# A four-layer graph network on one core: the input sums of one fast-multiplication pair are placed earlier in layer 2, and the weight sums of the last layer are placed behind four layer norms

## The chip, the cores and the metric

The kernel is one program for one NeuronCore of a Trainium2 chip. The metric is the device time of one execution in microseconds. A core has five engines that run side by side, each working through its own queue in order: TensorE (PE, matrix products into PSUM, with weight loads listed as PEld), VectorE (DVE), ScalarE (ACT), GpSimd (POOL) and SyncE (SP), which here only issues DMA transfers. An engine that needs another's result waits on a semaphore, and everything behind the waiting instruction waits too.

## The reference

The input `x` has 128 graphs of 64 nodes with 256 features, with one adjacency matrix for all. Four layers follow each other, and each ends with `x = layernorm(x + layer(x))`:

```python
# layer 0: graph attention with a dense mask
Wh = x @ W;  e = leaky_relu(Wh@a1 [:,None] + Wh@a2 [None,:]);  h = softmax(where(adj, e, -inf)) @ Wh
# layer 1: edge attention over 512 edges (src, dst), 4 heads, softmax per source node, then @ W_out.T
# layer 2: normalised adjacency, two linear layers with batch norms over all 8192 rows
agg = A_hat @ features
h   = relu(batchnorm(agg @ W1.T + b1))          # 256 -> 512
out = batchnorm(h @ W2.T + b2)                  # 512 -> 256
# layer 3: two graph convolutions, then LSTMs over windows of 1, 2, 3 and 4 nodes, in this order
h = relu(adj @ (x @ Wg0 + bg0));  h = relu(adj @ (h @ Wg1 + bg1))
for p in 1..4:
    last = lstm(Wih[p-1], Whh[p-1], windows of p nodes of h);  h[:, last node of each window] = last
```

All arithmetic is in 32-bit floats.

## The kernel before

The 8192 rows are worked on in 16 blocks `q` of 512 rows (`QT`), kept transposed in SBUF as `Aq(q)`: two halves of 128 features by 512 rows.

*Layers 0 and 1* run in a loop over blocks. The last steps of layer 1 for a block are three functions. `v_a` multiplies the values by the attention weights. `v_b` multiplies by the output weights, adds the old rows (L463, on DVE), makes the layer norm (statistics on DVE, L95 and L96; the power -0.5 on POOL, L86; four scalings on POOL, L100) and stores the block (`x2_dram`, an SP transfer at L467). `v_c` multiplies by the normalised adjacency (64 small products, L482) and writes the input of layer 2 into `Aq(q)`.

*Layer 2's first linear layer* makes `Z = W1 Aq` and gathers its batch-norm statistics (`bn_stats` on DVE). Seven blocks and the block `q = 11` are done plainly by `up_block` (products at L789). Pairs of neighbouring blocks (7 and 8, 9 and 10, 12 and 13, 14 and 15) use seven instead of eight block products (a Winograd form of Strassen's scheme). `Seven` holds such a job: `product(j)` multiplies (L860) and `use` combines the result with kept ones (`kept`, L872, and L885 and L888 on DVE; L870, L874, L876 and L879 on ACT; L880 and L886 on POOL). The product numbered 4 belongs to `tail`, which `seven` weaves into the next job.

The scheme needs four sums of a pair's inputs, made by `tile_sums`: three on POOL (`t3`, `t2`, `t4`, at L116 in the profile because all pass through the helper `given`) and one on DVE, in place (`t1`, written into `Aq`). Each pair takes one of two `rooms` in turn; pair 12 takes `[gath, lb, keep]`, so that `t3` is `lb`, `t2` is `gath` and `t4` is `keep`. Pair 7 had the same room.

The nine steps that finish layer 1 (`v_a`, `v_b`, `v_c` for blocks 13, 14, 15) alternate with nine entries of `fill`: five plain blocks, then `pair(7, 0)`, `pair(7, 1)`, `pair(9, 0)`, `pair(9, 1)`. The sums of pair 7 are made after the step n = 3, those of pair 9 after n = 5. Pair 12's are made when the loop is over, ahead of `up_block(11)`. After the loop SP also loads layer 3's weights and biases (`wg`, `bg`, `wih`, `bias`, `bias2`) into rooms that layer 1 leaves, and DVE adds the two biases (L1189).

*Layer 3* begins with four blocks (`parts`, generators made by `gcn`) that step through scaling, transposition, layer norms (two for each block, each with two stores `x3_dram` at L1338 and an `x2r` load of a later block at L1019), the small products with the adjacency (`neighbours`, L1295) and two linear layers (L1365, L1377). `first_sums` makes, once, four sums of the first LSTM's input weights on POOL (L1412) for the same seven-product scheme, and stores them (`sums1`), since the room is used for other weights afterwards and later pairs of block groups load them again. A list of block numbers gives the order in which the generators take their steps; `first_sums` stands before the list.

*What sets the order.* `given(do, ...)` issues a step so that on each of PE, DVE, ACT and POOL it comes after the instructions of the steps issued through `given` before it. Everything not pinned in this way, SP's transfers among it, is placed by the framework's scheduler, from the order in the code and from when it expects operands to be ready.

## Time and profile before

| | |
|---|---|
| median of 3 runs | 2028.21 us (2027.94 to 2029.69) |
| profiled execution | 2025.54 us |
| its span, first to last instruction | 2023.8 us |
| granted TensorE clock, mean | 0.986 |
| PE busy | 1934.4 us (96%) |
| DVE, ACT, POOL busy | 1277.3, 951.1, 881.1 us |
| DMA | 173.83 MB, mean 86 GB/s |
| chain that ended last | PE 77%, DVE 14%, ACT 4% |

The span is counted from the first to the last instruction of the profiled execution; the execution's own time is 1.74 us longer. Busy time is what an engine spent in instructions; the chain that ended last is followed back from the last instruction to whatever released each step. The granted clock is the share of TensorE's full clock; where it falls to 0.5, a product takes twice as long. A time in a profile line is in us from the start of the span, its second number is how long the merged instructions took, and the bracket at the end tells how long the engine had been idle and who ended that.

Layer 1's last steps and layer 2's pairs lie at about 555 to 640 us, layer 3 begins at about 745 us, and the LSTM steps fill the rest from about 785 us.

### The profile page before, as it was taken

What the parts mean: (1) busy time and instruction counts of PE and PEld (TensorE: products, weight loads), DVE (VectorE), ACT (ScalarE), POOL (GpSimd) and SP (SyncE); (2) the same over time, 40 slices, a digit from 0 to 9 for tenths busy, and PEclk for the clock granted to TensorE, in tenths of its full rate; (3) what the DMA queues carried; (4) which work ended last, traced back from release to release, by engine and by line L of the source; (5) the groups of instructions that cost most, each with busy time, mean ns of one, the idle gap of its engine ahead of it and who ended that gap; (6) DMA issues with size and microseconds to landing.
All of it is one profiled execution on the core that took longest, in us unless ns stands there. A gap on an engine that the chain in (4) does not pass through costs nothing.

```text
span 2023.8 us, 31384 instructions
## 1 busy us (share of the span) xinstructions
PE 1934.4 (96%) x11447; PEld 1336.6 (66%) x11447; DVE 1277.3 (63%) x2855; ACT 951.1 (47%) x1666; POOL 881.1 (44%) x1020
## 2 busy tenths in 40 slices
PE   5999999998999989899999999999999999999997
PEld 4667777776554445477678577678577668578685
DVE  7567776664556554765566765557865557764566
ACT  2666656665346523644333644343644333543333
POOL 1133343343444632664545544445543445444264
PEclk8999999999999989999999999999999999999998
DMA  5344443332311134432342233133243032131022
GB/s 141 72 68 69 82 79 55 56 56 45 45 46 27 42 132 144 177 125 94 120 141 84 101 124 136 42 130 93 64 146 118 19 115 70 41 120 79 0 63 73
DMA packets 236539, 173.83 MB, mean 86 GB/s; under 512 B 150625, under 2 KB 213601, under 8 KB 233057
## 3 DMA queue, kind: packets, MB, share of 16 engines
q1 hardware_dynamic: 234528, 169.86, 29.6%
q8 instruction: 90, 1.47, 0.3%
q0 software_dynamic: 1024, 1.05, 0.2%
q10 hardware_dynamic: 832, 0.92, 0.1%
q14 instruction: 65, 0.52, 0.1%
HBM read 110.18 MB, written 61.60 MB: 85 GB/s over the span
## 4 chain that ended last, share of the span: by engine, by line
PE 77%; DVE 14%; ACT 4%; issue 2%; POOL 1%; DMA 1%; SPq 0%; DVEq 0%; POOLq 0%; ACTq 0%
PE l L1743 29%; PE l L1699 8%; PE pz L860 4%; PE l L1478 4%; PE m L338 3%; PE pz L789 3%; PE m L257 3%; PE e L367 3%; PE z L376 2%; PE m L461 2%; PE m L341 2%; PE g L1377 2%; PE g L1365 2%; PE pz L1058 2%; DVE cell L1657 1%
## 5 line engine op out<-in xcount | busy, mean ns | idle before, releaser
L1743 PE MATMUL l<-hs,wh 128*128 128x256 f32 (+1 forms) x896 | 276.0, 399 | 3.7 <-DVE hs L1607 3.1
L1743 PE MATMUL l<-xs,wx 128*128 128x256 f32 (+1 forms) x896 | 276.0, 399 | 2.8 <-DVE gate L1762 2.8
L1758 ACT ACTIVATE kept<-l 128x256 f32<-128x256 f32 (+1 forms) x224 | 88.6, 402 | 333.6 <-PE l L1743 332.2
L86 POOL TENSOR_TENSOR ln_rs<-ln_rs,mhalf 128x2 f32<-128x2 f32 (+2 forms) x98 | 85.9, 876 | 344.2 <-DVE ln_rs L98 338.6
L1743 PE MATMUL l<-H,wx 128*128 128x256 f32 (+1 forms) x672 | 210.5, 402 | 4.3 <-DVE gate L1771 3.4
L1743 PE MATMUL l<-hid,wh 128*128 128x256 f32 (+1 forms) x672 | 208.8, 399 | 0.0
L1743 PEld LDWEIGHTS l<-hs,wh 128*128 128x128 f32 x896 | 169.1, 190 | 47.1 <-DVE hs L1607 5.7
L1743 PEld LDWEIGHTS l<-xs,wx 128*128 128x128 f32 x896 | 168.9, 190 | 45.8 <-POOL st L100 2.7
L1699 PE MATMUL l<-H,wx 128*128 128x256 f32 (+5 forms) x672 | 185.0, 431 | 4.9 <-DVE H L116 2.7
L1776 ACT ACTIVATE gate<-gate,bias 128x512 f32<-128x512 f32 (+1 forms) x280 | 170.5, 657 | 40.6 <-DVE gate L1767 34.8
L378 ACT ACTIVATE u<-z 128x1024 f32<-128x1024 f32 x128 | 130.0, 1025 | 71.9 <-PE z L376 71.3
L1699 PEld LDWEIGHTS l<-H,wx 128*128 128x128 f32 x672 | 118.8, 190 | 65.3 <-issue 34.7
L1743 PEld LDWEIGHTS l<-H,wx 128*128 128x128 f32 x672 | 125.7, 190 | 42.6 <-DVE gate L1771 7.4
L1743 PEld LDWEIGHTS l<-hid,wh 128*128 128x128 f32 x672 | 127.2, 190 | 32.0 <-issue 2.9
L1766 POOL TENSOR_TENSOR gate<-gate,kept 128x256 f32<-128x256 f32 (+1 forms) x84 | 65.0, 774 | 145.3 <-DVE kept L1764 145.0
L1771 DVE TENSOR_TENSOR gate<-l,gate 128x256 f32<-128x256 f32 (+1 forms) x112 | 49.9, 446 | 87.6 <-POOL gate L1766 60.8
L349 DVE TENSOR_TENSOR qs<-m,qs 64x256 fp32r<-64x256 f32 x128 | 54.0, 422 | 76.5 <-ACT qs L348 74.4
L1611 POOL TENSOR_TENSOR hs<-hid 128x256 f32<-128x256 f32 (+1 forms) x28 | 26.0, 929 | 171.0 <-DVE hid L1643 87.9
L376 PE MATMUL z<-gath_r,qs 128*128 128x512 f32 x256 | 99.5, 477 | 0.6 <-ACT u L378 0.5
L1665 ACT ACTIVATE gate<-cell 128x512 f32<-128x512 f32 (+1 forms) x88 | 58.6, 666 | 82.6 <-DVE cell L1657 60.6
L1653 POOL TENSOR_TENSOR cell<-gate,cell 128x512 f32<-128x512 f32 (+1 forms) x56 | 75.3, 1366 | 28.2 <-ACT gate L1776 28.2
L1760 DVE TENSOR_TENSOR gate<-l,kept 128x256 f32<-128x256 f32 (+1 forms) x112 | 49.0, 438 | 59.9 <-ACT gate L1776 32.7
(386 smaller groups left out, 4079.4 us busy)
## 6 DMA issues: line engine op xcount, KB each, us to landing
wx<-sums SPq DMA_DIRECT2D x9, 2048.0 KB
wh<-sums SPq DMA_DIRECT2D x9, 1792.0 KB
way<-st SPq DMA_DIRECT2D x54, 256.0 KB
st<-way SPq DMA_DIRECT2D x216, 64.0 KB
xin<-in_x SPq DMA_DIRECT2D x16, 512.0 KB
ld<-table SPq DMA_DIRECT2D x16, 512.0 KB
x_dram<-y SPq DMA_DIRECT2D x16, 512.0 KB
x2r<-x_dram SPq DMA_DIRECT2D x32, 256.0 KB
```

What stands on the lines that cost most here:

```text
L86: nc.gpsimd.tensor_tensor(dst, dst, mhalf[:, :n], OP.pow)
L257: nc.tensor.matmul(p_, xT[:, k, c * P:(c + 1) * P], w0[:, k, :], start=k == 0, stop=k == KD - 1)
L376: nc.tensor.matmul(z[:, k, :], L1[q]["qs"][c][:, s, k * P:(k + 1) * P], gath_r, start=True, stop=True)
L378: nc.scalar.activation(u, z, AF.Relu)
L860: nc.tensor.matmul(self.bank[at], lhs, rhs, start=first and n == 0, stop=n == len(self.terms) - 1, skip_group_check=True)
L1478: nc.tensor.matmul(self.bank[at], lhs, rhs, start=new, stop=True, skip_group_check=True)
L1653: nc.gpsimd.tensor_tensor(c, t, c, OP.mult)
L1699: nc.tensor.matmul(b, w.raw[0][:, k, at, m, :], x, start=k == 0, stop=k == KD - 1)
L1743: nc.tensor.matmul(self.banks[j], lhs, rhs, start=src == 0, stop=src == 1)
L1758: nc.scalar.activation(self.keep(j), b, AF.Copy)
L1766: e.tensor_tensor(t[0][:, 1], t[0][:, 1], k[5], OP.add)
L1776: given(lambda: nc.scalar.activation(dst, dst, f, bias=b))
```

## The change

In layer 2, `tile_sums` is split: the generator `sums_in_two` issues `t3`, `t1` and `t2` in a first part and `t4` in a second, and `tile_sums` runs both at once for the pairs that keep their place. For pair 12 the first part is issued after the step n = 6 (`v_a` of block 15 and `pair(7, 1)`), the second after n = 7 (`v_b` of block 15 and `pair(9, 0)`). Later `T` takes over the finished list.

In layer 3, `first_sums` is issued after the seventh step in the list of block steps (the `None`), which is behind the first four layer norms; its store becomes a function of its own, `keep_sums`, and is called after the list.

```diff
-        def tile_sums(b):
+        def sums_in_two(b):
 
             t2, t3, t4 = rooms[next(rooms_at) % len(rooms)]
             t1 = b(0, 1)
             given(nc.gpsimd.tensor_tensor, t3, b(1, 1), t1, OP.subtract)
             given(nc.vector.tensor_sub, t1, t1, b(0, 0))
             given(nc.gpsimd.tensor_tensor, t2, b(1, 1), t1, OP.subtract)
+            yield
             given(nc.gpsimd.tensor_tensor, t4, b(1, 0), t2, OP.subtract)
-            return [t1, t2, t3, t4]
+            yield [t1, t2, t3, t4]
+
+        def tile_sums(b):
+            both = sums_in_two(b)
+            next(both)
+            return next(both)
...
             if n in sums_at:
                 T[sums_at[n]] = tile_sums(inputs(sums_at[n]))
+            if n == 6:
+                end_sums = sums_in_two(inputs(NQ - LAST))
+                next(end_sums)
+            elif n == 7:
+                T[NQ - LAST] = next(end_sums)
...
-        T = {ends[0]: tile_sums(inputs(ends[0]))}
+        T = {ends[0]: T[ends[0]]}
         given(up_block, q)
...
             nc.gpsimd.tensor_tensor(S[:, dst], x, y, op)
+
+    def keep_sums():
+        S = rooms_of(0)[1]
         d = dram.tile([P, 3 * QT], F32, name="sums1")
         nc.sync.dma_start(d, S.rearrange("p j g c -> p (j g c)"))
         sums_kept.append(d)
...
-    given(first_sums)
-    for n in [0, 0, 0, 1, 1, 0, 1, 0, 0, 1, 2, 0, 0, 2, 1, 2, 1, 0, 3, 1, 1, 1]:
-        given(next, parts[n])
+    for n in [0, 0, 0, 1, 1, 0, 1, None, 0, 0, 1, 2, 0, 0, 2, 1, 2, 1, 0, 3, 1, 1, 1]:
+        given(*(first_sums,) if n is None else (next, parts[n]))
+    keep_sums()
```

## The prediction

> **What bounds the kernel now.** I read the page first. TensorE is busy almost throughout and the chain that ended last is mostly its own work, so time can only be won where PE stands still or runs at a reduced clock.

> ```profile
> PE 1934.4 (96%) x11447; PEld 1336.6 (66%) x11447; DVE 1277.3 (63%) x2855; ACT 951.1 (47%) x1666; POOL 881.1 (44%) x1020
> PEclk8999999999999989999999999999999999999998
> ```

> Then I read the chain of waits around the end of layer 1 beside layer 2, where the diff moves `tile_sums`. Columns: start, length, who.

> ```profile
> 596.61 2.16 POOL y L100 x4
> 598.77 1.23 POOL lb L116
> ...
> 600.81 1.27 POOL gath L116
> 602.08 1.23 POOL Z L880
> 603.30 1.23 POOL keep L116
> 604.53 1.23 POOL Z L886
> ...
> 606.40 0.68 DVE kept L872
> ...
> 607.13 1.12 PE pz L860 x2
> ```

> POOL runs the last norm (`y`), and then the three sums of pair 12 (`lb`, `gath`, `keep`) interleaved with pair 9's additions (`Z`). The last addition releases a DVE statistic, that one DVE's `kept` sum, and that one the product `seg` on PE. PE's timeline shows 2.31 us of idle before 607.13, put down to `kept L872`. The stretches just behind it (length, busy us of PE, PEld, DVE, ACT, POOL, then the granted clock) show a second loss:

> ```profile
> 606.00:608.00 2.00, 0.87 (x2) 0.49 (x3) 1.97 (x4) 0.00 (x0) 1.86 (x3) 1.00 0.92 265
> 608.00:610.00 2.00, 2.00 (x4) 0.86 (x3) 1.64 (x3) 0.00 (x0) 1.98 (x3) 0.60 0.96 17
> 610.00:612.00 2.00, 2.00 (x4) 0.74 (x3) 0.70 (x1) 0.57 (x1) 2.00 (x2) 0.55 0.81 6
> ```

> The clock costs 0.40 x 2 + 0.45 x 2 = 1.7 us. Third, POOL's and PE's timelines at the start of layer 3:

> ```profile
> 748.45 1.97 POOL L1412 TENSOR_TENSOR wh<-wih 128x384 f32<-128x384 f32 x2 [1.98 <-PE g L1327]
> 750.49 0.99 POOL L1412 TENSOR_TENSOR wh<-wh,wih 128x384 f32<-128x384 f32 x1
> 751.57 0.99 POOL L1412 TENSOR_TENSOR wh<-wih,wh 128x384 f32<-128x384 f32 x1
> 752.52 0.70 POOL L86 TENSOR_TENSOR ln_rs<-ln_rs,mhalf 128x2 f32<-128x2 f32 x1
> ```
> ```profile
> 753.93 1.25 PE L1295 MATMUL g<-bdT,A 64*64 64x64 f32 x32 [3.47 <-POOL A L100]
> 755.82 1.25 PE L1295 MATMUL g<-bdT,A 64*64 64x64 f32 x32 [0.64 <-POOL A L100]
> ```

> `first_sums` (L1412) holds POOL for 4.1 us; the first norm's power stands behind it and PE waits 3.47 us for that norm.

> **Part 2, the sums of layer 3 behind four norms.** Same four POOL additions, moved. DVE's first L85 ran at 750.08 and took 0.36 us, ending with POOL's addition; alone it takes 0.17 (770.72). So the power can start at 750.35 instead of 752.52. It takes 0.70, and the two L100 (1.09) end at 752.25. The second norm was ready on DVE at 752.14; its L85 will again wait for POOL's L100 (to 752.25), so its power starts near 752.5, and its first L100 ends at 752.5 + 0.70 + 0.10 + 0.55 = 753.85, against 755.77 now. PE's second group of 32 moves from 755.82 to 753.9: **1.9 us**. From 755.82 to 800 PE is idle for less than 1 us in all, so nothing there takes it back. Norms three and four follow at 754.6 and 758.1; the four additions then fill 760 to 764, where POOL sat idle for 8.95 us (to 770.97) and will be wanted near 769. DVE's work in that stretch (L1367) read PSUM and took 0.69 beside a busy POOL at 761.70, so I charge nothing. If that cover failed, up to 4 us of the fifth norm's lead would go.

> On SP the store of the sums (0.32 us to issue) used to stand before eight `x_dram` stores, and the four `x2r` loads behind all eight. In the new order each pair of stores is followed by its load, then the sums' store (now waiting for POOL at 764), the load of `WhhT` (748.32 before, about 764 after), one `z_dram` load and the `x3r` loads. The `x2r` loads come up to 10 us earlier, but no wait of DVE or PE on them shows now, so that is worth nothing. `WhhT` is first needed by L1244 at 831.28: 60 us of cover. What queues behind the store until 764 was issued at 764.4 to 767.2 before.

> **Part 1, pair 12's sums two places sooner.** The same four subtractions. On POOL `lb` now stands between pair 7's two additions, `gath` after them, `keep` behind the norm. On DVE the subtraction in place stands before the two sums L463 of the last norm. Step by step:

> - POOL: L880 ends at 589.88 as now; `lb` 589.84 to 591.11; L886 from 591.07 (589.84 now).
> - DVE's subtraction is released by `lb` at 591.15, after POOL began L886. Both read two operands from SBUF. The nearest row for that:

> ```profile
> 841.35 2.38 DVE L116 TENSOR_TENSOR wh<-wh,hs 128x512 f32<-128x512 f32 x2 [0.19 <-ACT wh L116]
> ```
> ```profile
> 841.31 1.27 POOL L116 TENSOR_TENSOR gate<-wx,gate 128x512 f32<-128x512 f32 x1 [0.47 <-ACT wh L116]
> ```

> Two such DVE operations take 1.29 us alone (818.64) and 2.38 when POOL began 0.04 earlier: the first was held until POOL ended. So ours ends at 592.9. Behind it: L463, a statistic, L463, and the norm's statistics, now at 592.94, then at 594.65. The norm is 1.7 us late (d = 1.7). Bounds: not held, d = 0.6 (the statistic between the two sums still waits for L886 until 592.34); held by `gath` as well, which waits for it, is excluded. I take 1.7, by the row.
> - POOL's L100 ends at 600.5 instead of 598.77. PE's 64 products on `y` (598.00 to 599.28) end at 600.85: it waits about 1.6 us here.
> - Behind the norm only `keep` and the two `Z` additions are left: 600.5 + 3 x 1.23 = 604.2; statistic, then `kept` at 604.85, done 605.5. PE reaches `seg` at 600.8 + 5.25 (its present distance, 599.22 to 604.66, less a 0.1 wait) = 606.05. The stall is gone; `seg` runs 1.1 us sooner, the reduced clock saves 1.7: PE is 2.8 ahead.
> - What is late next:

> ```profile
> 613.14 0.19 DVE L1189 TENSOR_TENSOR bias<-bias,bias 128x32 f32<-128x32 f32 x1 [2.44 <-DMA bias<-in_L_gnn_bhh]
> ```

> DVE is in order, and this addition waits for two bias loads. SP issues them behind `x_dram<-y` (issued when the norm ends, 599.1) and `wih`, which waits until that store has landed (603.8); all of this moves by d, to 614.85. Behind the addition stand six statistics and sums of 0.6 and one of 0.77, and the next `kept`: 5.2 us, so 620.05. Now PE, not DVE, was late there (619.50). PE wants that `kept` for the product at 622.07 - 2.8 = 619.3 and gets it at 620.1. Then DVE's in-place subtraction and POOL's `wv` (1.26) let the product at 623.79 start at 622.0: **1.8 us** sooner, in general 3.55 - d.

> From there to 743 PE has one wait of 0.19 us, so 1.8 is kept. [...] The row has the fall behind 2.31 us (0.60, 0.55), and idles of 1.91 (133.04), 2.09 (78.46) and 2.24 (471.94) fell too, while 1.77 (830.06) did not. I go by the rows. By the same rows the new wait at 598 to 600.85, about 1.65 us in pieces, stays just below.

> **Sum.** 1.8 + 1.9 = 3.7 us. The profiled execution took 2025.54 (span 2023.8 and 1.74 outside); its successor would take 2021.8. The median of the runs lies 2.67 above it, which I carry over: 2028.21 - 3.7 = 2024.5.

> **Rivals.**

> - *The port does not hold DVE* (0.32), or the clock falls less often. d = 0.6: part 1 gives 2.9 and the sum 4.8: 2023.4, down to 2022 with one more window of full clock. For it: the hold rests on 0.08 us of order.
> - *Layer 2 gives nothing* (0.12). The broken wait at 598 drops the clock (up to 1.7 us, of which 0.7 is slack before the bias load decides), or the dip at 608 is missing in most runs of before. Then only part 2 counts: 1.9, 2026.3, to 2028 with a slow return of the clock in layer 3.
> - *The bias loads become the bound* (0.11, slower). Place: DVE's addition, now 613.14. Price: 1 us per us of delay, and 1.7 when PE stands long enough to lose its clock. Part 1 loses from d = 3.55, the whole change from about 3.8 (5.5 without the clock). For it: the loads move single elements (DMA 0.96 busy at 17 GB/s), and they are tied to a norm that this change delays. Against: nothing adds traffic there, and d is bounded by one POOL addition. With a delay of 10 us: 6.45 + 1.7 - 1.9 = 6.2 slower, 2034.4.
> - That the change does nothing is excluded: the order of POOL, DVE and SP differs as described; PE's and ACT's are unchanged.

> **Numbers.** The main case has 0.45, at 2024.5 (2023 to 2026). Over 0.2% (4.1 us, about what a measurement of this kernel can tell from no change) means below 2024.1: a third of the main case, nearly all of the first rival: 0.46. Slower by 0.2%: the bias case, 0.11. Between: 0.43. The range, 2022.0 to 2028.0, leaves out the bias case and the ends of the others.

> **What would show it.** `lb` near 590, before pair 7's last addition; DVE's subtraction beside it 1.75 us long (0.69: first rival); L100 ending at 600.5; no idle before `seg`; granted clock 1.00 from 606 to 612; DVE's bias addition near 614.9 and PE idle about 0.8 us before the `lb` product that follows. In layer 3: power at 750.4, L1295 near 751.8 and 753.9, 4 us of L1412's successors from 760. Wrong: a bias wait beyond 617, a reduced clock behind 601, or PE waiting for the fifth norm.

## The result, and the profile after

The changed kernel took 2020.34 us (median of 8 runs, 2017.79 to 2023.74), and the kernel before, run beside it, 2028.08 (8 runs, 2023.16 to 2030.43). The ratio is 0.9968, with a 95% interval of 0.9957 to 0.998: 4 to 9 us faster. The forecast was 2024.5, with a range down to 2022.0. The direction was right, the mechanisms in the main too, and the time lies below the range. The sections below put the change at 3 to 5 us, near the 3.7 of the forecast, and the usual time of before at about 2024.8 instead of the 2028.2 that the sum started from. In this first comparison before ran at 2028 all the same, and why is not shown.

The changed kernel's profiled execution took 2020.14 us (span 2018.4). The page, busy time and granted clock:

```profile
PE 1933.2 (96%) x11447; PEld 1337.6 (66%) x11447; DVE 1277.1 (63%) x2855; ACT 951.8 (47%) x1666; POOL 884.7 (44%) x1020
PEclk8999999999999989999999999999999999999998
```

PE's busy time fell by 1.2 us, the span by 5.4. Busy time alone would not show where: a product at half clock counts as busy for twice as long (in before, L789's products start 0.86 us apart at a granted clock of 0.5, at 608.62 and 609.48, and 0.43 us apart at full clock, at 612.36 and 612.79).

**A point of reference first.** The two profiles are already 1.92 us apart at pair 7's addition L880 (588.61 before, 586.69 after), ahead of every instruction that the change moves. The clock explains most of it. In the first 100 us the granted clock fell to 0.5 in before at 24.72, 38.38, 52.03 and 79.34 us, for 3.41 us each and 6.83 at 38.38, and in the changed kernel at 22.58 and 39.65, for 6.83 us each: 17.1 us in all against 13.7. The 3.41 us more cost up to 1.7 us, half of them, by my estimate. So below I give distances from two markers inside one profile: from pair 7's L880 on POOL for layer 2, and from the scaling's power (`sc`, L86 on POOL) for layer 3.

**Layer 2.** The chain of waits in the changed kernel (start, length, who):

```profile
587.96 1.24 POOL lb L116
...
589.26 1.63 issue
590.89 0.68 DVE y L463
...
596.35 2.18 POOL y L100 x4
...
604.78 7.78 DMA bias<-in_L_gnn_bhh
...
612.65 0.19 DVE bias L1200
...
617.84 7.37 PE pz L860 x16
```

In before this chain ran over POOL's additions, `kept` and `seg`. Those are gone from it. In their place stand the subtraction on DVE that is held (1.63 us in which nothing else shows), the norm, and behind `seg` the bias load. PE's timeline in before, then in the changed kernel, and the stretches behind `seg` (length, busy PE, PEld, DVE, ACT, POOL, granted clock, DMA):

```profile
607.13 1.12 PE L860 MATMUL pz<-seg,SW 128*128 128x512 f32 x2 [2.31 <-DVE kept L872]
608.09 3.30 PE L789 MATMUL pz<-A,w 128*128 128x512 f32 x4
...
623.79 1.02 PE L860 MATMUL pz<-wv,SW 128*128 128x512 f32 x2
```
```profile
596.96 2.07 PE L482 MATMUL m<-aht,y 64*64 64x64 f32 x64 [0.81 <-POOL y L100]
604.21 1.02 PE L860 MATMUL pz<-seg,SW 128*128 128x512 f32 x2
605.07 1.88 PE L789 MATMUL pz<-A,w 128*128 128x512 f32 x4
617.84 1.12 PE L860 MATMUL pz<-lb,SW 128*128 128x512 f32 x2 [0.32 <-DVE kept L872]
...
619.79 1.12 PE L860 MATMUL pz<-wv,SW 128*128 128x512 f32 x2
```
```profile
604.00:606.00 2.00, 2.00 (x6) 0.83 (x5) 1.97 (x4) 0.93 (x2) 1.92 (x3) 1.00 0.75 184
606.00:608.00 2.00, 2.00 (x6) 0.88 (x5) 0.78 (x2) 0.69 (x1) 2.00 (x3) 1.00 1.11 219
```

The 2.31 us of idle before `seg` are gone, and so is the clock of 0.60 and 0.55: L789's four products take 1.88 us instead of 3.30. PE now waits earlier, for the late norm, and later, before the product on `lb` (0.32). The wait for the norm is 0.81 us ahead of the 64 small products and goes on inside them: they start in groups of 16, each behind one of POOL's four scalings, 0.54 us apart instead of 0.28, so the merged line reads 2.07 us where before had 1.28. The granted clock is 1.00 there, and one product takes 0.22 us in both. From L880, `seg` starts at +17.52 (before +18.52) and the product on `wv` at +33.10 (before +35.18): 2.1 us.

**Layer 3.** The scaling's power and the first LSTM products in before:

```profile
745.93 0.54 POOL L86 TENSOR_TENSOR sc<-sc,mhalf 128x1 f32<-128x1 f32 x1 [6.32 <-DVE sc L85]
```
```profile
785.34 7.03 PE L1546 MATMUL l<-H,wih 128*128 128x512 f32 x16
```

POOL's and PE's timelines in the changed kernel:

```profile
742.06 0.54 POOL L86 TENSOR_TENSOR sc<-sc,mhalf 128x1 f32<-128x1 f32 x1 [6.32 <-DVE sc L85]
747.10 0.70 POOL L86 TENSOR_TENSOR ln_rs<-ln_rs,mhalf 128x2 f32<-128x2 f32 x1 [4.50 <-DVE ln_rs L98]
```
```profile
744.02 2.03 PE L1338 MATMUL g<-ident,A 128*128 128x128 f32 x8
...
748.51 1.66 PE L1306 MATMUL g<-bdT,A 64*64 64x64 f32 x32 [1.61 <-POOL A L100]
750.52 1.24 PE L1306 MATMUL g<-bdT,A 64*64 64x64 f32 x32 [0.35 <-POOL A L100]
...
779.90 7.03 PE L1560 MATMUL l<-H,wih 128*128 128x512 f32 x16
```

The first norm's power stands at +5.04 from the scaling's (before +6.59), the second group of small products at +8.46 (before +9.89), and the first product of the LSTM at +37.84 (before +39.41). So the profiles show 2.1 and 1.6 us at the two places, and 1.9 ahead of both that do not belong to the change.

### The profile page after: what moved, and what is told of

Same layout as the page of the kernel before. It is cut to its first block, busy times and chain, and to the rows that moved or that the text cites. A ratio compares the mean times of both kernels' runs of the same rounds, so it can differ in the third digit from the quotient of the medians.

```text
span 2018.4 us, 31386 instructions
## 1 busy us (share of the span) xinstructions
PE 1933.2 (96%) x11447; PEld 1337.6 (66%) x11447; DVE 1277.1 (63%) x2855; ACT 951.8 (47%) x1666; POOL 884.7 (44%) x1020
## 4 chain that ended last, share of the span: by engine, by line
PE 76%; DVE 14%; ACT 3%; DMA 2%; issue 2%; POOL 1%; SPq 0%; DVEq 0%; POOLq 0%; ACTq 0%
PE l L1757 27%; PE l L1713 8%; PE l L1492 4%; PE pz L860 4%; PE m L338 3%; PE e L367 3%; PE z L376 3%; PE m L257 3%; PE m L341 3%; PE pz L789 2%; PE m L461 2%; PE g L1388 2%; PE pz L1069 2%; PE g L1376 2%; PE l L1560 1%
## 5 line engine op out<-in xcount | busy, mean ns | idle before, releaser
L86 POOL TENSOR_TENSOR ln_rs<-ln_rs,mhalf 128x2 f32<-128x2 f32 (+2 forms) x98 | 86.4, 882 | 343.5 <-DVE ln_rs L98 331.3
```

The lines of the kernel that those rows point to most:

```text
L86: nc.gpsimd.tensor_tensor(dst, dst, mhalf[:, :n], OP.pow)
```

## The experiments

The measures of all profiles in one table; a session is a set of runs made side by side on one chip. "seg" and "wv" are the starts of these products after pair 7's L880, "clock" tells whether it was reduced behind `seg` (L789's four products took 1.88 us where it is called full, 2.55 to 3.36 where reduced), "LSTM" is its first product after the scaling's power. The ratio is to before in the same session, with its 95% interval; medians of before were 2024.54, 2024.35, 2024.88 and 2025.90 in four sessions (e1 to e4, e5 to e8, e9 to e12, e13), each on another chip.

| kernel | seg | wv | clock | LSTM | median us | ratio |
|---|---|---|---|---|---|---|
| before | 18.52 | 35.18 | reduced | 39.41 | | |
| changed | 17.52 | 33.10 | full | 37.84 | 2020.34 | 0.9968 (0.9957 to 0.998) |
| e1 part 1 alone | 17.51 | 33.04 | full | 38.56 | 2021.96 | 0.9986 (0.9979 to 0.9992) |
| e2 part 2 alone | 18.54 | 35.08 | reduced | 38.01 | 2023.38 | 0.9993 (0.9984 to 1.0001) |
| e3 before again | 18.51 | 35.17 | reduced | 39.38 | 2026.24 | 1.0004 (0.9994 to 1.0013) |
| e4 bias addition later | 17.52 | 32.38 | full | 38.06 | 2020.35 | 0.9978 (0.9967 to 0.9988) |
| e5 idle filled, 4 products | 19.67 | 35.13 | full | 39.31 | 2023.81 | 0.9998 (0.9989 to 1.0007) |
| e6 store alone | 18.53 | 35.19 | reduced | 38.81 | 2023.97 | 0.9997 (0.9989 to 1.0005) |
| e7 subtraction behind the norm | 16.77 | 31.73 | full | 36.48 | 2019.02 | 0.9971 (0.996 to 0.9982) |
| e8 layer 3 filled, 12 products | 17.52 | 32.38 | full | 37.82 | 2021.60 | 0.9988 (0.9981 to 0.9995) |
| e9 changed again | 17.51 | 32.57 | full | 37.72 | 2020.67 | 0.9976 (0.9966 to 0.9986) |
| e10 idle filled, 2 products | 18.52 | 35.13 | full | 39.26 | 2024.07 | 0.9998 (0.999 to 1.0006) |
| e11 layer 3 filled, 5 products | 17.51 | 32.37 | full | 36.18 | 2018.95 | 0.997 (0.9959 to 0.9982) |
| e12 e7 and e11 together | 16.79 | 31.76 | full | 34.99 | 2015.96 | 0.9961 (0.9948 to 0.9974) |
| e13 as e10, `wq` in its place | 18.52 | 33.49 | full | 38.50 | 2022.15 | 0.9983 (0.9977 to 0.999) |

### e1 and e2: the two parts alone

e1 is the diff of the change without its last two blocks (`first_sums`, `keep_sums` and the list stay as before); e2 is those two blocks alone.

> Part 1 alone (layer 2's sums earlier, layer 3 as before). Theory A (the two parts are local and add up; the rest of the measured 6 to 8 us is where TensorE's clock happened to be reduced in a run): from pair 7's L880 on POOL to the product on wv on PE 33.1 us instead of 35.18, so 2.1 us gained there, nothing gained or lost elsewhere, total about 2.1 us below before. Theory B (part 1 is worth more in most runs than in the profiled one, because the stall before seg usually costs more than one stretch of reduced clock): total 4 to 5 us below before. Theory C (the two parts only gain together): total within 1 us of before.

> Part 2 alone (layer 3's sums behind four norms, their store later; layer 2 as before). Theory A: from the scaling's power L86 to the first LSTM product 37.9 us instead of 39.41, total about 1.5 to 1.9 us below before; the stall of 2.3 us before seg and its reduced clock stay. Theory B: total 2 us below, and part 1 brings the larger rest. Rival D (the store's new place on SP brings more than POOL's order): the LSTM part behind 785 us is shorter too, total 3 us or more below.

Part 1 alone is 0.14% faster (1.6 to 4.3 us), part 2 alone 0.07% (the interval reaches from 3.2 us faster to 0.2 slower). The first reaches `wv` at +33.04, the second the LSTM at +38.01, as theory A had it, and 2.8 and 1.4 us add up to 4.2. Part 2's gain alone is not clear of noise in the total. Theory C falls with e1. Theory B's 4 to 5 us for part 1 lie at or beyond the end of its interval. Rival D falls in e6.

e1's layer 3 is the old one, and yet its LSTM begins at +38.56, 0.85 earlier than in before. No instruction was moved there; the halved clock lay elsewhere. In before's trace it lasted from 2.4 to 16.1 us after the scaling's power (748.35 to 762.00). In e1 the first two products of 128x128, 1.4 us after the power, took 0.77 us instead of before's 0.46, and the eight of 128x512 behind the small products 4.87 (3.67 at a clock of 1.00 in e12), from which I estimate that it ended 14.4 us after the power. The LSTM distance of one profile therefore has about a microsecond of chance in it. Seven profiles with the old order (before, e1, e3, e5, e6, e10, e13) have a mean of 39.0, five with the new order and no filling (changed, e2, e4, e7, e9) 37.6, a difference of 1.4 us. Where two profiles, one of each order, have stretches that, estimated from these eight products, end within 0.3 us of each other, it is less: 0.72 (e1 and changed), 0.78 (e13 and e9) and 0.75 (e6 and e4). So part 2 is worth 0.7 to 1.4 us there, and the rest of the difference is where the stretches fell.

### e3: before once more

Edit: none.

> The kernel before once more, nothing changed. It gives a second profile and the time and clock of each run. Theory A: ratio 1.000 within 0.1%; the places of reduced clock in the first 140 us differ from those of the first profile by one or two stretches of 3.41 us, each worth up to 1.7 us of span; the stretch behind the stall before seg (2.3 us idle) is there again. If the clock there stays full in this profile, the 1.7 us that the prediction booked for it is not gained in every run.

The reduced clock behind `seg` is there again. The stretches, then PE's timeline of this kernel:

```profile
609.00:611.00 2.00, 2.00 (x4) 0.85 (x3) 1.62 (x4) 0.00 (x0) 2.00 (x3) 0.56 1.08 22
611.00:613.00 2.00, 2.00 (x4) 0.83 (x3) 0.62 (x1) 0.61 (x1) 2.00 (x2) 0.58 0.86 6
```
```profile
608.03 1.12 PE L860 MATMUL pz<-seg,SW 128*128 128x512 f32 x2 [2.30 <-DVE kept L872]
608.99 3.36 PE L789 MATMUL pz<-A,w 128*128 128x512 f32 x4
```

The distances repeat those of before to 0.03 us. What does not repeat is the total: the 14 runs went from 2022.83 to 2031.18. Their time goes with the mean clock that each run lists: for before in the same session, 3 runs at 0.984 took 2029.0 us on average and 12 runs at 0.988 took 2023.7, some 1.3 us for each 0.001.

### e9: the changed kernel once more

Edit: none.

> The changed kernel once more, nothing altered. Theory A (the change is worth 3.6 us, as the two places in the profiles show, and the three runs of before that the prediction started from were slow ones): 3.0 to 4.5 us below before in the same call, ratio 0.998, its times 2020 to 2022 with before at 2024 to 2025; granted clock full behind seg. Theory B (the change is worth 6 to 8 us in most runs): ratio 0.9965 again.

Theory A: 2020.67 against 2024.88, 0.9976, which is 2.8 to 6.9 us. Theory B named 0.9965, just outside. The changed kernel repeated its first median to 0.3 us; what differs between the two comparisons is before, 2028.08 against 2024.88. Over the four sessions before ran 138 times, with a median of 2024.76 and nine runs in ten between 2021.5 and 2028.9. All three runs that the forecast started from lay at 2027.94 or above, where only 10 of the 138 lie. Of the five further runs of before in the first comparison three lay high as well (2027.35 to 2030.43) and two did not (2023.16, 2023.91).

### e4: the bias addition later

```diff
         nc.sync.dma_start(z_dram[q], Aq(q))
-        nc.vector.tensor_add(bias, bias, bias2)
...
     keep_sums()
+    given(nc.vector.tensor_add, bias, bias, bias2)
     lstms = [lstm(k) for k in range(NP)]
```

> The changed kernel with the addition of the two LSTM biases moved from layer 2's end to behind layer 3's block steps on DVE. Theory A (in the changed kernel PE is 2.8 us ahead until DVE waits 5.47 us for the bias load, which takes 0.7 of it back): no DVE wait at 612, no PE wait before the product on lb, from pair 7's L880 to the product on wv 32.4 us (33.10 in the changed kernel), total 0.7 us below the changed kernel. Rival (the subtraction in place and wv on POOL are late anyway, or the loads slow the rest): 33.1 again, total as the changed kernel.

As expected: `wv` at +32.38, 0.72 sooner than in the changed kernel. DVE and PE of e4:

```profile
615.98 0.69 DVE L872 TENSOR_TENSOR kept<-pz,kept 128x512 f32<-128x512 f32 x1 [0.37 <-PE pz L860]
```
```profile
618.55 1.02 PE L860 MATMUL pz<-lb,SW 128*128 128x512 f32 x2
```

Now `kept` waits for PE and PE no longer waits for `kept`. The wait for the bias load was thus what capped part 1 in the changed kernel's profile. It is a small cap: in e9 the same product on `lb` came without a wait and `wv` at +32.57. The 0.7 us cannot be told in the totals (2020.35 against 2020.34 and 2020.67).

### e5, e10 and e13: PE's idle before seg filled

```diff
             def multiply(self, j):
...
+                if j == 7 and self.fill:
+                    for _ in range(4):
+                        lhs, rhs = factor(1, *self.terms[0])
+                        nc.tensor.matmul(self.bank[0], lhs, rhs, start=True, stop=True, skip_group_check=True)
```

`fill` is true for one job, `pair(9, 1)`. e5 has four products and the bias addition moved, on the kernel before; e10 has two products and the same move; e13 adds an order on DVE:

```diff
-            job.counted(0, 1)
+            with tc.issue_after(job.added) if job.fill else ExitStack():
+                job.counted(0, 1)
```

where `added` is the sum that writes `wq`. The bias addition was not moved alone on the kernel before. In before's trace PE does not wait from `seg` to the product on `wv`, so the move by itself has nothing to free there.

> The kernel before (bias addition moved behind layer 3's block steps) with four products of 128x512 (0.43 us each, their result is not used) put on PE ahead of the product on seg, where it stands idle for 2.3 us. The wait itself stays. Theory A (the idle of 2.3 us brings the stretch of reduced clock behind it, which is the 1.7 us term of part 1): seg still 18.5 us after pair 7's L880, granted clock 1.00 behind it, the product on wv at 33.5 us instead of 35.2, total about 1.7 us below before. Rival (an idle of 2.3 us is too short to lower the clock, something else does): reduced clock behind seg as before, product on wv at 35.2, total as before.

> As the kernel with products put into PE's idle before seg, with two of them instead of four (each turned out to be two passes, 0.86 us together, so four lasted 3.5 us and made seg 1.15 us late). Theory A (the idle brings the reduced clock): seg at 18.5 us after pair 7's L880, no reduced clock behind it, product on wv at 33.5 to 34.0 us, total 1.2 to 1.7 us below before. Rival (two products leave 0.6 us of idle, and the clock falls all the same, or DVE's wq sets the pace): product on wv at 35.2 us.

> As the kernel with two products in PE's idle before seg, with wq kept ahead of the block's statistic on DVE, as in before (in the run with two products the two had changed places, wq came 1.4 us too late and the next product waited for it). Theory A (a full clock behind seg is worth its 1.7 us when nothing else stops PE): seg at 18.5 us after pair 7's L880, no wait for wq, product on wv at 33.4 us instead of 35.2, total 1.7 us below before. Rival (without the reduced clock PE only runs into the next wait, so this term of the prediction's sum is worth nothing on its own): product on wv at 34.5 us or more.

e5 missed its aim in one respect: one product shows as two of the trace's matmuls, 0.43 us apart, so four lasted 3.5 us (eight matmuls in 3.70) and `seg` came 1.15 late. The clock behind it stayed full (L789's four in 1.88 us). e10 had `seg` on time and a full clock, and gained nothing. PE's timeline of e10 (the lines of the job stand six lower there: L860 is L866, L872 is L878) shows who took it back:

```profile
605.15 1.12 PE L866 MATMUL pz<-seg,SW 128*128 128x512 f32 x2 [0.42 <-DVE kept L878]
606.12 1.88 PE L789 MATMUL pz<-A,w 128*128 128x512 f32 x4
609.37 1.12 PE L866 MATMUL pz<-w,w 128*128 128x512 f32 x2 [1.38 <-DVE wq L891]
```

The scheduler, which saw two more products, had put a statistic ahead of `wq` on DVE. With `wq` kept in its place (e13) PE runs on:

```profile
610.55 1.13 PE L866 MATMUL pz<-seg,SW 128*128 128x512 f32 x2 [0.41 <-DVE kept L878]
611.51 1.88 PE L789 MATMUL pz<-A,w 128*128 128x512 f32 x4
613.23 1.02 PE L866 MATMUL pz<-w,w 128*128 128x512 f32 x2
```

`wv` comes at +33.49 instead of +35.18, the 1.7 us expected; the ratio gives 2.0 to 4.7 us, a little more than the place shows. This shows the clock term. In these profiles the idle before `seg` brought the reduced clock (full in the three profiles in which the idle was filled, reduced in the four in which it was not), and the full clock, with nothing else in PE's way, is worth 1.7 us. The idle of 2.30 or 2.31 us was followed by the reduced clock four times in four; in before it ended at 607.13, and the stretch lasted from 608.40 to 611.82.

### e6: the store alone

`keep_sums` is split off and called behind the list as in the change; `given(first_sums)` stays ahead of the list.

> The kernel before with only the store of layer 3's sums issued behind the list of block steps (SP's order as in the changed kernel, the sums on POOL where they were). Theory A (part 2's gain comes from POOL's order alone): the first norm's power 6.6 us after the scaling's, PE's wait for the first norm 3.5 us, first LSTM product 39.4 us after the scaling's power, total within 0.1% of before. Rival D (the earlier x2r loads and the late store bring part of it): first LSTM product at 38.9 us or less, total 0.5 us or more below.

The power stays at +6.59 and the second group of small products at +9.89, both as in before, and the total is 0.9997. The LSTM at +38.81 is below the line that rival D drew, but behind an unchanged start: the eight products of L1365 took 5.12 us there instead of 5.70, so less of them ran at half clock. SP's new order is worth nothing that can be seen.

### e7: nothing of pair 12's sums before the norm

```diff
-            return lambda: up_job(q, g, T[q])
+            return lambda: up_job(q, g, T[q], **dict(order=given) if (q, g) == (7, 1) else {})
...
             given(nc.gpsimd.tensor_tensor, t3, b(1, 1), t1, OP.subtract)
+            if apart:
+                yield
             given(nc.vector.tensor_sub, t1, t1, b(0, 0))
...
             given(do, q, *[False] * (do == v_c))
+            if n == 7:
+                next(end_sums)
```

and the bias addition as in e4.

> The changed kernel with the bias addition moved, POOL's lb pinned behind pair 7's last addition, and the subtraction in place behind the last norm's statistics, so that nothing of pair 12's sums stands before that norm (d = 0 in the prediction's sum); gath moves behind the norm, where four additions then stand instead of three. Theory A (part 1 is what it would be without the delay of the norm, less that delay): last L100 ends 10.2 us after pair 7's L880 instead of 11.8, products on y wait no longer, seg at 16.5 us (17.5 in the changed kernel), product on wv at 31.3 us (33.1), total 1.8 us below the changed kernel, 5.4 below before. Rival (with gath behind the norm the additions end too late again and seg waits for kept): seg at 17.5 us with an idle of 1 us or more, total as with the bias addition moved alone.

DVE's and POOL's timelines, then PE's:

```profile
595.72 0.68 DVE L116 TENSOR_TENSOR A<-A 128x512 f32<-128x512 f32 x1
```
```profile
595.82 1.46 POOL L86 TENSOR_TENSOR ln_rs<-ln_rs,mhalf 128x4 f32<-128x4 f32 x1 [2.93 <-DVE ln_rs L98]
```
```profile
605.94 1.12 PE L860 MATMUL pz<-seg,SW 128*128 128x512 f32 x2 [0.54 <-DVE kept L872]
```

The subtraction takes 0.68 us again, the norm ends 10.37 us after L880 (10.16 in before), `seg` is at +16.77 and `wv` at +31.73: 3.45 us sooner than in before. Theory A had 31.3; the difference is 0.54 us of idle before `seg`, since four additions now stand behind the norm, so the rival has its part, but a small one. Against e4, which has the same place for the bias addition, the norm ends 1.45 us sooner and `wv` comes 0.65 sooner. The delay of the norm, d, is a cost, as the prediction's sum had it, but here less than half of what was taken off it came back. The total, 2019.02, is 3.6 to 8.1 us below before.

### e8, e11 and e12: the clock at the start of layer 3

```diff
-    pr = gbank([P])
+    room = gbank([QT])
+
+    def warm(dst, n):
+        for _ in range(n):
+            nc.tensor.matmul(dst, ident, wih1[:, 0, :QT], start=True, stop=True, skip_group_check=True)
+
+    given(warm, room, 7)
+    pr = room[:, :P]
```

and the bias addition as in e4, and `warm` with 5 products into the first bank of `neighbours` before block 0's small products; their results are overwritten. e11 has 3 and 2 products instead of 7 and 5, e12 is e11 with e7's edits.

> The changed kernel with the bias addition moved and twelve products of 128x512 whose result is not used: seven on PE between layer 2's last product and layer 3's first, five ahead of the first group of small products (L1306 in the changed kernel), where PE waits for the norm. Theory A (the idle of 3.3 us at the start of layer 3 brings the 10 to 14 us of halved clock that follow, and part 2 was made within them): granted clock 1.00 from 742 to 757, first LSTM product 34 to 35 us after the scaling's power instead of 38, total 3 to 4 us below the version with the bias addition moved. Rival (the clock there is set by something else, or the later waits lower it all the same): reduced clock at the same place, first LSTM product at 38 us, total the same or up to 1 us more.

> As the kernel with twelve products in PE's idles at the start of layer 3, with three and two of them (2.6 and 1.7 us) so that they end before the real work is ready. Theory A: no reduced clock from 742 to 757, first LSTM product 35 to 36 us after the scaling's power (38 with the bias addition moved alone), total 2 to 3 us below that version. Rival (the remaining idles of 0.7 us and the short small products lower the clock after all): 37 us or more.

> The version with pair 12's subtraction behind the norm and lb behind pair 7's last addition, together with three and two products in PE's idles at the start of layer 3. Theory A (the gains add up): product on wv at 31.7 us, first LSTM product at 35 to 36 us after the scaling's power, mean clock 0.992, total 7 to 8 us below before, 3 to 4 below the changed kernel. Rival (the gains share one cause, so that one takes the other's): 5 us below before, as with the subtraction moved alone.

e8 had twice the intended length, for the reason found in e5: the clock stayed full (eight products of 128x512 in 3.67 us at 751.30, against 5.58 in the changed kernel), but the seven products held up the first transpositions (4.2 us after the scaling's power instead of 2.0) and the five made the first small products 2 us late, and nothing was won. e11's are short enough, and the norm comes sooner than in any version without them. POOL and PE of e11:

```profile
746.93 0.70 POOL L86 TENSOR_TENSOR ln_rs<-ln_rs,mhalf 128x2 f32<-128x2 f32 x1 [3.80 <-DVE ln_rs L98]
```
```profile
748.35 1.00 PE L1314 MATMUL g<-bdT,A 64*64 64x64 f32 x32 [0.30 <-POOL A L100]
750.34 1.08 PE L1314 MATMUL g<-bdT,A 64*64 64x64 f32 x32 [1.00 <-POOL A L100]
```

The power stands at +4.33 from the scaling's (742.60). One stretch of 3.41 us at half clock was left behind the idle of 1.00 us (from 751.12; granted clock 0.78, 0.50 and 0.87 in the three stretches of 2 us from 750), and the LSTM began at +36.18, 1.9 sooner than in e4; the intervals of the two totals (0.997 and 0.9978, in different sessions) overlap. In e12 no stretch was left (granted clock 1.00 from 736 to 752), and it began at +34.99. e12 is the best version: 2015.96 us, 5.3 to 10.5 us below before, and 4.7 below the changed kernel in the same session by the medians (their intervals against before, 0.9948 to 0.9974 and 0.9966 to 0.9986, still touch). The gains add up at the two places, `wv` as in e7 and the LSTM 1.2 us sooner than in e11; the totals are too near each other to show it.

## Why the prediction missed

**The step that failed** is the last one of the sum: "The median of the runs lies 2.67 above it, which I carry over: 2028.21 - 3.7 = 2024.5." That median came from three runs, and before's 138 later runs put it at 2024.76. The same 3.7 us from there give 2021.1, against measured medians of 2020.34 and 2020.67. The term was mis-sized by 3.4 us (2028.21 against 2024.76). The profiled execution, at 2025.54, was the better guide and stood in the text: 2021.8. The range failed with it, since it held the bounds of the unknown costs and nothing for the start. The first comparison itself does not show this: before ran at 2028.08 beside the changed kernel, and the ratio there, 4 to 9 us, leaves 3.7 out. The later sessions do not: 2.8 to 6.9 us in e9, and 4.2 as the sum of e1 and e2. For what goes beyond 4 to 5 us no profile shows a mechanism. Why those first runs of before took longer, and the changed kernel's beside them did not, stays open: the clocks of those eight runs are not on record. In the later sessions a longer time went with a lower mean clock (e3), which may hold here too.

**The steps of part 1**, in their order:

- d = 1.7: the last L100 ends 1.67 later than in before (+11.83 against +10.16). Right.
- The subtraction held, 1.75 us. POOL's and DVE's timelines of the changed kernel:

```profile
589.15 1.27 POOL L886 TENSOR_TENSOR A<-wq,kept 128x512 f32<-128x512 f32 x1
```
```profile
589.22 1.74 DVE L116 TENSOR_TENSOR A<-A 128x512 f32<-128x512 f32 x1 [0.53 <-POOL lb L116]
```

  So the first rival, in which DVE is not held, falls: beside no POOL addition the subtraction takes 0.68 (e7). What holds it, no trace names. Its other half, a clock that falls less often, has no support in the profiles: behind the idle before `seg` it fell four times in four. No run shows "one more window of full clock", the 1.4 us between 2023.4 and the range's 2022; what the runs show is the 1.7 us of e13.
- PE waiting 1.6 for the late norm: L482 ended 1.7 later. Right; half of it is one wait of 0.81, the rest lies between the groups of products.
- `seg` 1.1 sooner without a stall: 1.00. Right.
- The clock's 1.7: shown by e13. PE 2.8 ahead before the bias: 2.80 at the product before `lb` (616.39, against 621.11 less 1.92). Right.
- The bias wait: expected 0.8 us of idle, 1.8 left in all. Measured 0.32 and 2.1; in e9 none, and 2.6. The loss was booked 0.3 to 0.8 too large, since the bias addition came 1.43 later in relation to L880, not a full d, and in e9 0.89 later.

**Part 2** was booked as 1.9. Two of its steps were off. The first is "So the power can start at 750.35 instead of 752.52". It started 0.6 later than that in relation to the scaling (+5.04, not +4.42), and so the second group of small products is 1.4 us sooner instead of 1.9. In before's profile the first four transpositions still ran at full clock; in the changed kernel the reduced clock had begun (742.79, +0.7, against 748.35, +2.4: eight transpositions in 2.03 us, where before did the first four in 0.60), and DVE's first sum behind them came 0.63 later (+3.06 against +2.43). Before, then the changed kernel:

```profile
747.63 0.60 PE L1327 MATMUL g<-ident,A 128*128 128x128 f32 x4
```
```profile
748.36 0.68 DVE L1333 TENSOR_TENSOR x2r<-g,x2r 128x512 f32<-128x512 f32 x1
```
```profile
745.12 0.69 DVE L1344 TENSOR_TENSOR x2r<-g,x2r 128x512 f32<-128x512 f32 x1 [0.24 <-PE g L1338]
```

With POOL's sums out of the way that chain was last. e11, with a full clock, has +4.33, the forecast's value. In e1 and e13 the eight transpositions also took 2.03 us, and with the old order the power still stood at +6.59 and +6.58: the sums had covered this loss of the clock.

The second is "nothing there takes it back". PE's idle was counted, the clock was not: of the 1.4 us at the small products 0.7 to 0.8 are left at the LSTM in the three pairs of profiles with like stretches (e1 and e2).

The errors, part 1 too low by 0.3 to 0.8 and part 2 too high by 0.5 to 1.2, nearly cancel, and that is luck. The other rivals: layer 2 gave something, and the bias loads became the last wait, as feared, but at 0.7 us (e4).

## What to carry to other kernels

Before summing gains of 4 us, find out what the kernel's own runs differ by, and start from the profiled execution or from many runs, not from three. Compare two profiles by distances between instructions near the change, since the same code ahead of it can be 2 us apart. Where an idle of PE is followed by a reduced clock, a few products without use in that idle can win more than the shorter wait itself (e13 won 1.7 us; without the wait `seg` starts only 1.0 sooner), if they end before the real work is ready and the scheduler's order on the other engines is kept.
